# A gated cross-attention and FFN layer: where the first norm's statistics are taken, how the query weights get their mean, and TensorE transposes of the identity at two seams

## The chip, the cores and the metric

The kernel runs on one core of a Trainium2 chip. The metric is the device time of one execution in microseconds. The engines of the core are TensorE (PE: matrix products and transposes), VectorE (DVE), ScalarE (ACT), GpSimd (POOL) and SyncE (SP), which here only issues DMA copies. Each engine works through its own instructions in order and waits on semaphores for the others.

## The reference

x has 4 batches of 1024 tokens of 512 elements, the context 4 batches of 64 tokens. One layer of cross-attention (16 heads of 64) and one quantized feed-forward layer are added, each behind a layer norm and scaled by the tanh of a gate:

```python
scores = einsum('bhqd,bhkd->bhqk', q, k) * SCALE            # q = split(norm(x) @ w_q)
scores = scores + (1.0 - mask) * -10000.0                   # causal: only the first 64 tokens see less
out = softmax(scores) @ v ; return merge(out) @ w_o         # k, v from ctx

x = act_qdq(x)                                              # the FFN: whole-tensor 16 bit levels
up   = act_qdq(x @ lpbq_dequant(w_up).T)                    # weights: 4 bit in blocks of 32
gate = act_qdq(x @ lpbq_dequant(w_gate).T)
sig  = fixed_qdq_u16(sigmoid(gate))
o = act_qdq(act_qdq(gate * sig) * up)
return o @ lpbq_dequant(w_down).T

x = x + tanh(g_xattn[0]) * xattn(layernorm(x), ctx, ctx, ...)
x = x + tanh(g_ffn[0]) * ffn(layernorm(x), ...)
```

The first norm's mean and variance of each token are needed for the attention, the second norm's for the feed-forward layer.

## The kernel before, in words

The 4096 tokens are 32 tiles of 128 (NT), in 8 groups of 4 tiles (NG, GRP) or 16 pairs of tiles (NQ; 4 pairs to a batch). All is in float32.

**Setup (0 to 77 us).** The weights are loaded. As q and k meet only in the scores, the query weights are multiplied into the keys beforehand: for each of 8 pairs of heads (hp), TensorE turns the pair's query weights into PSUM (`query_turned`, L535), DVE takes the mean of each row by batch-norm statistics and an aggregation and writes the difference into `wqT` (L547), and TensorE multiplies by the keys (L566) into five PSUM banks (`ps_mm`), which ACT (10 copies for each hp, L577) and DVE (6, L579) empty into `m_all`. In the same way the values are multiplied into the output weights (`value_matrix`, L605, emptied by ACT at L611 and DVE at L613 into `vwo`). Since the mean is taken out of the query weights, the first norm needs only the factor `rstd1`, one number for each token; it scales the scores inside the softmax. Its statistics (`group_stats`: batch-norm statistics L324 and an aggregation L327 for each tile) come from copies of x, one of 1 MB (`xe`) for each group: groups 0, 1 and 2 behind the head pairs 3, 5 and 6, in the order of the program, groups 3 and 4 among the value products. At L745 `norm_of` turns the variances of groups 0 to 4 into `rstd1`: an addition (L175) for each group and several small instructions on DVE, with a square root on ACT (L178), whose table must be loaded. All that `norm_of` issues has a raised priority.

**Attention (77 to 546 us).** For each pair q, TensorE computes the scores of pair q+1 (seven products, as in Strassen's scheme, L411), and between them turns the weights of pair q (`weights_turned`, L656); it then multiplies these by the values (`attend`, seven products, L690). ACT or DVE add each product into `e` (L417, L419). The softmax takes maxima, exponentials (ACT, L449, 32 for a pair, with a table of its own) and a division (DVE, L455). Four additions on DVE (L662 to L665) prepare the turned weights `eT` for the scheme; L663 is used below as the mark of a pair. `attend` adds its result to the tokens `xg` (L698) and takes the second norm's statistics (L324). `renormed` scales a tile by the second norm (ACT, L718; DVE for the last two, L723), turns it (L731) and keeps it for the next stage. The last pairs of each group end with `norm_of` for the second norm of that group. For groups 5, 6 and 7 the first norm's statistics are taken from `xg` in the pairs 7, 9 and 11, when `xg` has been loaded, and their norm is joined to the second norm's `norm_of` of those pairs. DVE also does the dequantization of the gate and up weights and the sums of the scheme meanwhile.

**Gate (553 to about 870 us), up (to 1146) and down (1151 to 1449).** The three products of the feed-forward layer, with the quantization between them. Before the down stage TensorE turns its weights (`down_turned`, L246; ACT empties each, L248). The largest values over all tokens are needed before a stage's integers can be made. This makes two seams at which TensorE has little to do: between attention and gate, and between up and down.

**The order.** In attention and in the feed-forward layer TensorE's order is that of the program. The other engines' orders are made by a planner from the program and from priorities: `high_priority(SOON)` moves instructions ahead, `issue_after` places them behind a given instruction, `keep_in_program_order` fixes them. Copies into SBUF are issued on SP's queue in that queue's order: a copy whose buffer is not yet free holds the copies behind it.

Of the kernel before, what the change touches and what calls it, by code (L numbers as in the profile page):

```python
# [7 lines left out]
F32 = mybir.dt.float32  # L8
# [9 lines left out]
P = 128  # L18
# [9 lines left out]
def kernel(  # L28
# [253 lines left out]
    def down_turned(psp):  # L282
        for cc in range(IC // 4):
            wdT.append(slot([P, 4, H], f"wdT{cc}"))
            for rc in range(H // P):
# [3 lines left out]
                )  # L289
                yield  # L290


    LO, HI = slice(0, HC // 2), slice(HC // 2, HC)
    LEFT, RIGHT = slice(0, HH), slice(HH, H)
# [27 lines left out]
    def stats(pool, src, dst, tag, in_order=False):  # L322
        st = pool.tile([P, 6], F32, name=f"st_{tag}", tag="st")
        ins = nc.vector.bn_stats(st, src)  # L324
        if in_order:
            tc.keep_in_program_order(ins)
        nc.vector.bn_aggr(dst, st)  # L327

    def group_stats(pool, g, x, in_order=False):
        for i in range(GRP):  # L330
            stats(pool, x[:, i, :], mv1[:, g * GRP + i, :], f"a{g}_{i}", in_order)

    def first_norm(*groups):
        return [(rstd1, None, mv1, of_group(g)) for g in groups]
# [124 lines left out]
    with tc.tile_pool(name="su", bufs=1) as su, tc.tile_pool(  # L459
# [75 lines left out]
        def query_turned(hp):  # L535
            ps = ps_tr.tile([P, 4, P], F32, name=f"ps_wq{hp}", tag="tr")
            for hc in range(HC):
                tc.keep_in_program_order(
                    nc.tensor.transpose(
                        ps[:, hc, :], wq[hp // 4][:, hc, (hp % 4) * P : (hp % 4 + 1) * P], ident  # L540
                    )
                )

            ps = ps.rearrange("p c n -> p (c n)")
            mean = su.tile([P, 2], F32, name=f"mean{hp}", tag="mean", bufs=2)
            stats(su, ps, mean, f"wq{hp}")
            nc.vector.tensor_scalar(  # L547
                wqT[hp // 4][:, hp % 4, :], ps, mean[:, 0:1], None, ALU.subtract
            )

        stats_at = (3, 5, 6)
        query_turned(0)
        left = {}
        for hp in range(HP):
# [29 lines left out]
            if hp in stats_at:  # L584
# [2 lines left out]
                nc.sync.dma_start(out=xe, in_=tokens_of(g))  # L587
                group_stats(su, g, xe, True)

        for b in range(2, B):  # L590
            for k in range(2):
                nc.gpsimd.dma_start(out=m_d[b][k], in_=m_all[b][k])
# [4 lines left out]
        left[0] = score_left(0)  # L597
        for _ in batch_sums(0, 0):
            pass
        def value_matrix(b, hp, ps):  # L600

            for j in range(2):
                half = slice(j * D, (j + 1) * D)
                to = j if b % 2 == 0 else 1 - j
                nc.tensor.matmul(  # L605
                    ps[to * D : (to + 1) * D, :], vT[half, hp, b * KL : (b + 1) * KL],
                    wo[hp // 4][half, hp % 4, :], start=True, stop=True,
                )
            dst = vwo[b][hp // 4][:, hp % 4, :]
            if b != B - 1 or hp % 2 == 0:  # L610
                nc.scalar.activation(dst, ps, AF.Copy, scale=tanh_g[0])  # L611
            else:
                nc.vector.tensor_scalar(dst, ps, tanh_g[0], None, ALU.mult)  # L613

        for hp in range(HP):
            if hp in (0, 3):
                g = 3 + hp // 3
                xe = pa.tile([P, GRP, H], F32, name=f"xe_{g}", tag="e")
                nc.sync.dma_start(out=xe, in_=tokens_of(g))
                group_stats(su, g, xe)  # L620
            for b in range(2, B):
                value_matrix(b, hp, ps_mm.tile([P, H], F32, name=f"ps_vo{b}_{hp}", tag="mm"))
                if hp % 4 == 3:
                    nc.gpsimd.dma_start(out=vwo_d[b][hp // 4], in_=vwo[b][hp // 4])
# [3 lines left out]
    with tc.tile_pool(name="ps_s", bufs=1, space=PSUM) as ps_s, tc.tile_pool(  # L628
# [113 lines left out]

        sg_t, ag = [], []
        last = NT - GRP
        norm_of(pa, first_norm(*range(5)), "a1")  # L745
        load_four(xf, 1, xb, "x")

        def next_left(q):
# [10 lines left out]
        next(firsts)  # L759
        next(firsts)  # L760
        softmax(0, ahead)
        for q in range(NQ):
            b, k = divmod(q, QPB)
            turns = weights_turned(q, ahead)
# [30 lines left out]
                    renormed(t - GRP)  # L795
            if q % 2 == 1 and q // 2 + 2 < NG:
                load_group(q // 2 + 2)
                if q // 2 + 2 > 4:
                    group_stats(pa, q // 2 + 2, xg[q // 2 + 2])
            if q + 1 == NQ:  # L800
                for p in range(UPB - 2):
                    ag.append(weight_sums(wgT, sg_t, p, "g"))
# [1 line left out]
            with tc.issue_after(added):  # L804
                if b + 1 < B and k in (1, QPB - 1):
                    for _ in batch_sums(b + 1, k // 2):
                        pass

            if q == NQ - 2:
                norm_of(pa, [second_norm(slice(last, last + 2))], "c0")  # L810
            if q % 2 == 1 and q + 1 < NQ:
                g = q // 2
                parts = [second_norm(of_group(g))]
                if 4 < g + 2 < NG:
                    parts += first_norm(g + 2)
                norm_of(pa, parts, f"b{g}")

            if 0 < q <= IC:
# [16 lines left out]
        renormed(last + 1)  # L835
        for t in (NT - 1, NT - 2):
            norm_of(pa, [second_norm(slice(t, t + 1))], f"c{t}")
        renormed(NT - 1)
        renormed(NT - 2)
    pools.close()  # L840

    s_x, inv_x = act_scale(over_all([am_x], "x"), None, "x")

    with tc.tile_pool(name="praw", bufs=RAW) as praw, tc.tile_pool(
# [183 lines left out]
        with tc.tile_pool(name="pc", bufs=2) as pc, tc.tile_pool(  # L1028
# [208 lines left out]
            load_early()  # L1237

            turn = down_turned(ps_tr)
            next(turn)  # L1240
            half_of_last(0, 0)
            for step, half, n in zip(tail, ((1, 1), (0, 1), (1, 0)), (1, 0, IC - 2)):
                step()
                half_of_last(*half)
                for _ in range(n):
                    next(turn)


    pe = ctx.enter_context(tc.tile_pool(name="pe", bufs=3))
# [280 lines left out]
```

## Time and profile before

| | us |
|---|---|
| median of 3 runs | 1455.46 (1454.54 to 1455.81) |
| the profiled execution | 1454.49 |
| its span, first to last instruction | 1452.7 |
| TensorE busy | 1395.7 (96%) |
| VectorE busy | 1163.4 (80%) |
| ScalarE busy | 683.2 (47%) |
| GpSimd busy | 96.4 (7%) |
| mean granted TensorE clock | 0.989 |

The page counts the time in which an engine executes; a busy engine may still execute slowly. The views of the waits name, for each engine, the line and buffer that stood, the engine and the line that ended the wait, the total in us, the number and the longest of them. The views of windows give the busy time of each engine in a stretch and, behind them, the granted TensorE clock as a share of full speed, the share of the DMA engines and the GB/s moved.

### The profile page before, as it was taken

The numbers are of one execution on the slowest core, as the hardware profiler recorded it, in microseconds if no ns is written. First come the engines' busy times: TensorE is split into PE (matmuls) and PEld (weight loads), VectorE is DVE, ScalarE is ACT, GpSimd is POOL, SyncE is SP. The second block draws the span as 40 slices with busy tenths as digits, with TensorE's granted clock in tenths as the row PEclk, the third lists the DMA queues.
The fourth block names the chain that finished last, engine by engine and source line by source line (L and its number), as shares of the span: only waits on it lengthen the run. The fifth ranks groups of instructions, "written<-read, shape, count | busy, mean of one in ns | idle before, by whom it ended". The sixth has DMA issues, their size and how long they took to land. (4 is left out here: it accounts for less than half of the span.)

```text
span 1452.7 us, 15275 instructions
## 1 busy us (share of the span) xinstructions
PE 1395.7 (96%) x4816; PEld 847.4 (58%) x4816; DVE 1163.4 (80%) x2165; ACT 683.2 (47%) x1639; POOL 96.4 (7%) x191
## 2 busy tenths in 40 slices
PE   8889999999899988999999999999999899999999
PEld 6526766766567674444444444344444448888887
DVE  3967989898898898799986579888888897666632
ACT  2545786677568852000000049987885532222200
POOL 0000000000000001000000000000000110111110
PEclk9999999999989999999999999999999999999999
DMA  9872344545504315692323448958557475554321
GB/s 282 292 200 68 73 145 108 154 136 116 155 27 123 115 27 214 177 376 87 130 87 116 145 151 340 362 217 318 218 217 260 178 287 174 185 188 173 134 73 44
DMA packets 189513, 249.57 MB, mean 172 GB/s; under 512 B 125300, under 2 KB 125556, under 8 KB 183412
## 3 DMA queue, kind: packets, MB, share of 16 engines
q1 hardware_dynamic: 163956, 146.84, 32.5%
q0 software_dynamic: 18560, 76.56, 13.7%
q10 hardware_dynamic: 6912, 25.17, 4.3%
q8 instruction: 38, 0.62, 0.2%
q14 instruction: 47, 0.39, 0.1%
HBM read 139.47 MB, written 109.05 MB: 171 GB/s over the span
## 5 line engine op out<-in xcount | busy, mean ns | idle before, releaser
L449 ACT ACTIVATE e<-e,mx,rstd 128x64 f32<-128x64 f32 x416 | 177.1, 429 | 8.9 <-DVE mx L447 8.8
L867 PE MATMUL pqup<-t,wuT 128*128 128x512 f32 x192 | 91.1, 597 | 5.1 <-DVE raw_up L888 2.9
L411 PE MATMUL s<-t,xs 128*128 128x512 f32 x192 | 91.7, 600 | 0.2 <-DVE e L419 0.2
L883 ACT COPY raw_gate<-ppgate 128x512 f32<-128x512 f32 x24 | 14.1, 586 | 143.5 <-PE ppgate L867 143.5
L449 ACT ACTIVATION_READ_ACCUMULATOR e<-e,mx,rstd 128x1 f32 x416 | 78.8, 190 | 0.0
L1397 PE MATMUL ep<-wdT,upe 128*128 128x256 f32 x336 | 77.1, 379 | 0.0
L1323 ACT ACTIVATE uie<-upe,inv_up 128x1024 int16<-128x1024 f32 x48 | 53.6, 1144 | 46.7 <-DVE upe L1327 27.4
L419 DVE TENSOR_TENSOR e<-s,e 128x512 f32<-128x512 f32 x80 | 54.6, 682 | 23.4 <-PE s L411 22.9
L1397 PE MATMUL eq<-tw,upe 128*128 128x256 f32 x312 | 72.4, 379 | 0.0
L1397 PEld LDWEIGHTS ep<-wdT,upe 128*128 128x128 f32 x336 | 63.8, 190 | 9.1 <-issue 0.5
L867 PE MATMUL ppup<-xu,wuT 128*128 128x512 f32 x144 | 67.7, 592 | 0.0
L1128 ACT ACTIVATE ar<-raw_up 128x1024 f32<-128x1024 f32 x46 | 48.3, 1053 | 40.1 <-DVE raw_up L1052 40.1
L1061 DVE TENSOR_REDUCE am_gu<-raw_up 128x1 f32<-128x512 f32 x92 | 62.5, 683 | 5.5 <-ACT raw_up L883 4.0
L867 PEld LDWEIGHTS pqup<-t,wuT 128*128 128x128 f32 x192 | 35.6, 189 | 52.6 <-issue 32.5
L411 PE MATMUL s<-m_all,xs 128*128 128x512 f32 x128 | 61.7, 613 | 4.4 <-DVE s_a L183 3.4
L690 PE MATMUL oq<-t,eT 128*128 128x256 f32 x256 | 61.0, 381 | 5.0 <-DVE xg L698 3.7
L875 ACT COPY raw_gate<-ppgate 128x512 f32<-128x512 f32 x24 | 14.1, 586 | 109.2 <-PE ppgate L867 72.7
L1397 PEld LDWEIGHTS eq<-tw,upe 128*128 128x128 f32 x312 | 59.3, 190 | 8.1
L1327 DVE SCALAR_TENSOR_TENSOR upe<-uie,inv_o,gse 128x1024 f32<-128x1024 int16 (+1 forms) x50 | 60.7, 1240 | 3.7 <-ACT uie L1323 3.5
L867 PE MATMUL pqgate<-t,wgTb 128*128 128x512 f32 x128 | 60.2, 592 | 0.0
L411 PEld LDWEIGHTS s<-t,xs 128*128 128x128 f32 x192 | 35.5, 193 | 41.5 <-issue 39.6
L1106 DVE SCALAR_TENSOR_TENSOR q<-gi,inv_gs,si 128x1024 int16<-128x1024 int16 x44 | 56.3, 1281 | 3.6 <-ACT si L1099 2.9
(342 smaller groups left out, 3136.0 us busy)
## 6 DMA issues: line engine op xcount, KB each, us to landing
gate_d<-raw_gate ACTq DMA_DIRECT2D x48, 512.0 KB, 2.6
gt<-gate_d SPq DMA_DIRECT2D x48, 512.0 KB, 4.6
upe<-up_d SPq DMA_DIRECT2D x24, 1024.0 KB, 6.3
up_d<-raw_up POOLq DMA_DIRECT2D x46, 512.0 KB, 3.6
gse<-gsi_d SPq DMA_DIRECT2D x24, 512.0 KB, 4.3
gsi_d<-q SPq DMA_DIRECT2D x44, 256.0 KB, 3.1
wxT<-in_x_dram SPq DMA_DIRECT2D x128, 64.0 KB, 2.8
xg<-in_x_dram SPq DMA_DIRECT2D x8, 1024.0 KB, 5.5
```

The costliest lines, as they stand in the source:

```text
L411: nc.tensor.matmul(bank[at], a[k][:, h, :], b[k][:, h, :], start=start and h == 0, stop=h == HC // 2 - 1, skip_group_check=True,)
L419: nc.vector.tensor_tensor(dst, bank[at], other, add)
L449: nc.scalar.activation(ei[:, h, :], ei[:, h, :], AF.Exp, bias=mx[:, h : h + 1], scale=root, accum_out=sm[:, h : h + 1],)
L690: nc.tensor.matmul(bank[at], a[k][:, h, :], b[k][:, h, :], start=start and h == 0, stop=h == HP // 2 - 1, skip_group_check=True,)
L867: nc.tensor.matmul(bank[at], a[k][:, h, :], b[k][:, h, :], start=start and h == 0, stop=h == HC // 2 - 1, skip_group_check=True,)
L875: nc.scalar.copy(r0[:, 1, :], bank["pp"])
L1061: nc.vector.tensor_reduce(am_gu[:, c, u : u + 1], r[:, c, :], AX.X, ALU.max, apply_absolute_value=True,)
L1106: nc.vector.scalar_tensor_tensor(gsi[u], gi, c_gs, si, ALU.mult, ALU.mult)
L1128: nc.scalar.activation(ar, raw[u], AF.Abs)
L1323: nc.scalar.activation(ui, up[:, i, :], AF.Copy, scale=inv_u)
L1327: ins = nc.vector.scalar_tensor_tensor(o[:, i, w], ui[:, w], c_o, gs[:, i, w], ALU.mult, ALU.mult)
L1397: nc.tensor.matmul(bank[at], a[u // 2][k][:, u % 2, q % 2, :], w_of[u // 2][k][:, u % 2, :], start=start and u == 0, stop=u == UPB - 1, sk ...
```

## The change

It has three parts.

1. **The first norm's statistics.** In setup only groups 0 and 1 are taken, behind head pairs 2 and 5; the norm of group 0 follows the loop over head pairs. A new `stats_of(g)` loads the four tiles of a group by four copies of 256 KB into two rotating buffers `xe` and takes the statistics of each. It is called for groups 2 and 3 behind the last value product that DVE empties (the planner may issue them only after it), and for groups 4 to 7 in the pairs 0 to 3, behind `attend`. The norm of groups 1 to 3 follows the first softmax; that of groups 4 to 7 is joined to the second norm's in pair 5. The statistics from `xg` in the pairs 7, 9 and 11 are gone, so x of the groups 5 to 7 is read once more than before.
2. **The mean of the query weights.** ACT copies the turned weights out of PSUM and sums each row on the way; DVE subtracts the sum over 512, in place.
3. **Transposes of the identity.** `keep_going` issues n TensorE transposes of the 128x128 identity into a PSUM tile which nothing reads: 12, 10 and 18 around the last two `renormed` tiles, and 7, 7 and 14 around the last two turns of the down weights.

TensorE's other instructions keep their order. On DVE, ACT and SP the planner arrives at another order in the setup and in the attention; in the later stages only some of ACT's and SP's instructions at the second seam change places. SP issues 363 rows in place of 336.

```diff
+    def keep_going(ps, n):
+        for _ in range(n):
+            nc.tensor.transpose(ps[:, :P], ident, ident)
...
+    def stats_of(g):
+        for i in range(GRP):
+            xe = pa.tile([P, H], F32, name=f"xe{g}_{i}", tag="xe")
+            nc.sync.dma_start(out=xe, in_=tokens_of(g)[:, i, :])
+            stats(pa, xe, mv1[:, g * GRP + i, :], f"e{g}_{i}")
...
-            ps = ps.rearrange("p c n -> p (c n)")
-            mean = su.tile([P, 2], F32, name=f"mean{hp}", tag="mean", bufs=2)
-            stats(su, ps, mean, f"wq{hp}")
-            nc.vector.tensor_scalar(
-                wqT[hp // 4][:, hp % 4, :], ps, mean[:, 0:1], None, ALU.subtract
+            total = su.tile([P, 1], F32, name=f"total{hp}", tag="total", bufs=2)
+            w = wqT[hp // 4][:, hp % 4, :]
+            nc.scalar.activation(
+                w, ps.rearrange("p c n -> p (c n)"), AF.Copy, accum_out=total
             )
-        stats_at = (3, 5, 6)
+            nc.vector.scalar_tensor_tensor(
+                w, total.to_broadcast([P, H]), -1.0 / H, w, ALU.mult, ALU.add
+            )
+        stats_at = (2, 5)
...
+        norm_of(su, first_norm(0), "a0")
         for b in range(2, B):
...
+                on_vector.append(nc.vector.tensor_scalar(dst, ps, tanh_g[0], None, ALU.mult))
         for hp in range(HP):
-            if hp in (0, 3):
-                g = 3 + hp // 3
-                xe = pa.tile([P, GRP, H], F32, name=f"xe_{g}", tag="e")
-                nc.sync.dma_start(out=xe, in_=tokens_of(g))
-                group_stats(su, g, xe)
...
-        norm_of(pa, first_norm(*range(5)), "a1")
         load_four(xf, 1, xb, "x")
...
         softmax(0, ahead)
+        with tc.issue_after(on_vector[-1].ins):
+            for g in (2, 3):
+                stats_of(g)
+        norm_of(pa, first_norm(1, 2, 3), "a1")
         for q in range(NQ):
...
                 load_group(q // 2 + 2)
-                if q // 2 + 2 > 4:
-                    group_stats(pa, q // 2 + 2, xg[q // 2 + 2])
...
+            if q < NG - 4:
+                stats_of(q + 4)
...
                 parts = [second_norm(of_group(g))]
-                if 4 < g + 2 < NG:
-                    parts += first_norm(g + 2)
+                if q == 5:
+                    parts += first_norm(*range(4, NG))
...
+        idle = ps_s.tile([P, H], F32, name="idle", tag="s0")
+        keep_going(idle, 12)
         renormed(NT - 1)
+        keep_going(idle, 10)
         renormed(NT - 2)
+        keep_going(idle, 18)
...
+            idle = ps_g.tile([P, TB], F32, name="idle_c", tag="pn")
             next(turn)
             half_of_last(0, 0)
             for step, half, n in zip(tail, ((1, 1), (0, 1), (1, 0)), (1, 0, IC - 2)):
                 step()
                 half_of_last(*half)
-                for _ in range(n):
+                for k in range(n):
+                    if k in (IC - 4, IC - 3):
+                        keep_going(idle, 7)
                     next(turn)
+            keep_going(idle, 14)
```

## Prediction

> **What bounds the kernel now.** I read the page first: the busy shares, then the waits of TensorE (PE), then short windows around the largest waits with the granted clock, last VectorE (DVE) instruction by instruction there.
>
> ```profile
> span 1452.7 us, 15275 instructions
> ...
> PE 1395.7 (96%) x4816; PEld 847.4 (58%) x4816; DVE 1163.4 (80%) x2165; ACT 683.2 (47%) x1639; POOL 96.4 (7%) x191
> ```
>
> PE is busy for 96% of the span: 57 us are left in which it does nothing, and its clock. The change leaves PE's products as they are, so it can only win there.
>
> ```profile
> PE ps_xm L731 <- ACT xm L718: 9.2, 1, 9.2
> PE ps_e L656 <- DVE e L455: 5.8, 4, 2.8
> ...
> PE ps_m L566 <- DVE wqT L547: 4.4, 3, 2.8
> ...
> PE s L411 <- DVE s_a L183: 3.4, 1, 3.4
> ...
> PE ps_vo L605 <- DVE vwo L613: 3.1, 2, 1.7
> PE ps_xm L731 <- DVE xm L723: 3.1, 2, 1.7
> ...
> PE ps_vo L605 <- ACT vwo L611: 0.9, 1, 0.9
> ```
>
> In setup PE waits for DVE (wqT, vwo, s_a). The largest wait of the run, 9.2 us from 393.6, stands in pair 10 of the attention, and ACT's xm there waits for DVE: the norm's chain runs from 394.19 (ve_b) to 401.73 (off), behind the statistics of group 7.
>
> ```profile
> 72.78:76.19 3.41, 1.18 (x12) 0.15 (x4) 2.94 (x8) 2.52 (x4) 0.00 (x1) 1.00 1.05 389
> 76.19:83.01 6.82, 5.61 (x7) 2.50 (x8) 1.54 (x9) 1.41 (x3) 1.06 (x2) 0.50 1.06 383
> 393.60:397.04 3.44, 0.00 (x0) 0.00 (x0) 3.44 (x13) 0.44 (x2) 0.00 (x0) 1.00 0.62 195
> 397.04:407.28 10.24, 4.53 (x15) 4.00 (x16) 10.24 (x26) 5.25 (x12) 0.00 (x0) 0.50 0.10 38
> 547.23:550.64 3.41, 0.86 (x6) 0.65 (x7) 3.20 (x15) 0.90 (x3) 0.02 (x1) 1.00 0.20 77
> 550.64:557.47 6.83, 4.75 (x9) 2.13 (x8) 6.21 (x18) 4.42 (x8) 1.08 (x3) 0.50 0.04 16
> 1141.15:1144.56 3.41, 2.82 (x22) 2.07 (x20) 2.72 (x9) 2.91 (x6) 0.37 (x1) 1.00 0.75 294
> 1147.98:1151.39 3.41, 0.69 (x5) 0.46 (x5) 2.11 (x8) 3.30 (x6) 0.57 (x1) 1.00 0.90 309
> 1151.39:1154.80 3.41, 3.41 (x4) 1.47 (x5) 3.38 (x6) 2.75 (x3) 1.65 (x3) 0.50 0.63 111
> ```
>
> The columns: length, busy us of PE, weight loads, DVE, ACT, POOL, then the granted clock. Each stretch at 0.50 follows a window of 3.41 us in which PE was busy for at most 1.18 us (0.35 of it). Two of them are the seams: end of attention (547 to 557) and gate and up into down (1148 to 1155).
>
> ```profile
> 77.00:121.00 44.00, 41.23 (x144) 15.89 (x144) 32.05 (x54) 20.36 (x41) 1.06 (x2) 0.93 0.74 169
> 121.00:229.00 108.00, 106.23 (x423) 72.55 (x424) 91.38 (x181) 76.39 (x289) 4.87 (x9) 1.00 0.36 89
> ```
>
> Here the first four pairs run: DVE has 12.0 and 16.6 us idle. What the change moves there has to fit into that.
>
> **The change, part by part.** The profiled execution took 1454.49 us (span and 1.8 around it), 0.97 under the median of 1455.46; the sum is made against 1454.49 and 0.97 is added. About 0.2% (2.9 us) is what a measurement can tell from no change.
>
> *1. Setup up to scores(0).* Removed from DVE: statistics of groups 2, 3, 4 (12 tiles at 0.69+0.18 = 10.4 us) and, in each of 8 head pairs, statistics and aggregation of the query weights (0.69+0.18); the subtraction (0.75) stays, in place. ACT takes a copy of 128x512 (0.59 for vT) with its row sum (the accumulator read is 0.19): 0.78 x 8 = 6.2 us, beside 16.0 us in which its m_all copies wait. The waits this can end: wqT 2.77+0.19, vwo 1.67+1.48, s_a 3.41, together 9.5; the 0.9 of ACT's vwo comes next, so 8.6 at most. New delays: DVE meets group 0's statistics after head pair 2 (about 37.2), when their 1 MB lands at about 39.3, holding the m_all copies behind them (PE about 1.4, since five banks cover the rest); the norm "a0" puts a table load (1.28) and a square root (0.2) on ACT ahead of a wqT copy (1.5); group 1's statistics (3.5) stand ahead of the last wqT (1.5 after slack). Together 4.4, so scores(0) gains 4.2 to 8.6.
>
> *2. scores(0) to the first turned weights (L663, first pair).* Before 77.4 to 120.5 = 43.1. The first two products took 3.75 and 2.90 us instead of 1.88 at half clock: 2.9 us go if PE no longer idles ahead of them. But DVE gets the 8 tiles of groups 2 and 3 and the norm of groups 1 to 3: two tiles and more fit before the first product ends (DVE idled 6.15 there), the six others (5.2) and the norm (1.5) do not; DVE's idle between reads up to 97 is 2.97+0.38+0.50+1.04 = 4.9. So about 1.8 us fall on PE. Two more table loads (2.6) lie in ACT's 24 idle us. Net 1.2. Steps 1 and 2: gain 5.4 to 9.8; I take 7.5, the middle, as each end rests on one wait.
>
> *3. The pairs.* Pairs 0 to 3 each get four tiles of statistics (4 x 0.87 = 3.5), groups 4 to 7. Pairs 7, 9 and 11 lose as much; the joined norm goes to pair 5. By rows, DVE's work between successive L663 is, before: 15.7, 24.1, 25.9, 23.6, 24.3, 24.0, 29.0, 28.6, 19.5, 22.9, 37.0, 23.8, 18.0, 28.9, 20.1 us; after, in the changed order: 22.2, 24.2, 29.4, 26.0, 27.7, 24.2, 29.7, 25.0, 19.5, 23.7, 29.3, 25.4, 16.9, 28.9, 20.1. PE's own period is 26.7 (25.8 for the first two, 20.1 for the last). With the larger of the two in each, before gives 408.8 (the trace has 413.2, so the order inside pairs costs 4.4 more) and after 403.6: 5.2 won. The long wait of pair 10 also ends its half clock: of 4.53 us of PE work in 397 to 407 half, 2.3, was the clock. I leave 0.6 of waiting there: 5.2+2.3-0.6 = 6.9. Bounds: 11 if the whole 9.2 and 2.3 go and DVE's idle 16.6 takes the new tiles almost free; 2 if each of the first four pairs loses 2 us more, because the softmax chain starts behind a statistic.
>
> *4. The copies.* Five copies of 1 MB become two and 24 of 256 KB (5 to 8 MB) on the sync queue. With two buffers each copy waits for DVE to be done with the one two before, and the queue waits with it: the x and gate weight loads behind it. The x rows of pairs 2 and 3 stand ahead of the first such wait; the others are used a pair (26 us) or more after their place, and 16 issues take 9 to 11 us there. Cost 0; without that slack DVE's first gate tile would stand in front of the softmax.
>
> *5. Seam 1.* 40 transposes around the last two tiles. In the trace 8 transposes take 0.87 us, so these 4.4 us fill a gap that PE waits out anyway (xm: 1.66+1.46). If they hold the clock, 4.75 us of work in 550.64 to 557.47 takes half, 2.4 less; but the second gate product waits for DVE's tile (ends 556.29), so I take 1.0, between 0 and 2.0.
>
> *6. Seam 2.* 28 transposes, 3.1 us, in a window with 0.69 us of work. PE is unbroken from 1151.35 to 1449.3, so all of the first window counts: 3.41 us at half clock, 1.7 less. Against it, 14 transposes (1.5) ahead of a turn may hold it; ACT's turned copy 1150.72 to 1151.30 ends last, so that is covered. The changed order also puts ACT's last turned copy, one uie (1.14 by its row) and SP's gse load ahead of the branch; at most 1.1 us either way for ACT, which was 97% busy in that window (3.30 of 3.41). POOL keeps its order but for one exchanged pair of stores. I take 1.6; bounds -1.5 and 1.7.
>
> In the window 1141.15 to 1144.56 PE did only transposes, and the next windows kept 1.00. The Trainium skill ("TensorE: Matmul & The Clock Gate", Part 4) says that in transpose mode the clock gate doesn't engage as it doesn't count as busy in the same way. By that rule steps 5 and 6 would be worth nothing; the trace's window, at 1.00, speaks against it.
>
> Sum: 7.5+6.9+1.0+1.6 = 17.0. 1454.49-17.0+0.97 = 1438.5.
>
> **Rivals.**
> A. *DVE is full in the first pairs.* For it: 29.4 and 27.7 in my list already pass PE's 26.7, and waits of PE for e-type tiles (5.8) show DVE late. Then step 3 gives 1 and steps 1 and 2 the low 5.4; with 2.6 of the seams 9.0: about 1446.5.
> B. *Transposes don't keep the clock up.* For it: the one window of transposes alone lies between windows of products, so it may have kept their clock, and the few transposes at seam 1 (six PE instructions in 547.23 to 550.64) did not stop the 0.50. Against it: that window itself. Then the 0.50 stays at both seams, and steps 5 and 6 go: 14.4 in place of 17.0, 1441.
> C. *Slower: every new statistic in pairs 0 to 3 falls on PE.* 24 tiles x 0.87 = 20.9 us, if PE always waits for the DVE read behind which a tile stands. Against it stand 28.6 us of idle DVE there. With the low gains (setup 4.2, pair 10 8.2, seams 2.6 = 15.0) the end is 5.9 later: 1461. It decides once more than 15.0 of the 20.9 us land on PE.
> D. *The part in pair 10 does nothing:* the chain of the second norm stays split by other DVE work, and the 9.2 us wait stays. For it: before, 7.5 us of chain held only 1.3 of its own instructions (0.12 to 0.20 each). Step 3 becomes 5.2-(37.0-29.3)+0 = -2.5: the sum is 7.6, about 1448.
> E. *Better:* every high end, 9.8+11+2.0+1.7 = 24.5: 1431.
>
> **How the numbers follow.** Forecast 0.50 (its own range 1432 to 1444), A 0.15, B 0.10, C 0.12, D 0.08, E 0.05. The range 1430 to 1450 takes in the centres of all but C; 0.12 for C and 0.08 for the tails of A, D and E lie outside. Slower by over 0.2%: C but for its mildest sixth, 0.10; within 0.2%: that sixth and the tails of A and D, 0.05; faster by over 0.2%: 0.85.
>
> **What would show it.** PE: no wait for s_a, and scores(0) beginning between 69 and 73; no 0.50 in the 7 us behind it. Pair 10: the wait for ACT's xm below 2 us, no half clock around 400. First pairs: distances of L663 of 25 to 30. Seams: rows "idle" in the windows that read 0.86 and 0.69 of PE work, and 1.00 in the windows after them. Wrong if PE waits for DVE's adds or weights in pairs 0 to 3 in sum by more than 10 us, if the xm wait stays, or if 0.50 stays at both seams.

## The result and the profile after

| | before | after |
|---|---|---|
| median of the runs beside each other (us) | 1455.07 | 1449.02 (1446.81 to 1452.2) |
| ratio, 95% interval | | 0.9956 (0.9943 to 0.997) |
| profiled execution (us) | 1454.49 | 1452.2 |
| its span | 1452.7 | 1450.4 |
| mean granted clock in it | 0.989 | 0.991 |

The kernel became faster by 6.05 us, where 17 were forecast. The profiled execution is the slowest of the five; the other four took 1446.8 to 1450.1 us at a mean clock of 0.993 or 0.994.

TensorE's share on the page of the changed kernel, and its three longest waits between 100 and 540 us (line, tile, who ended them; us in total, times, longest):

```profile
span 1450.4 us, 15457 instructions
...
PE 1406.2 (97%) x4884; PEld 857.6 (59%) x4884; DVE 1155.3 (80%) x2153; ACT 690.7 (48%) x1658; POOL 97.5 (7%) x191
```

```profile
PE oq L702 <- DVE xg L710: 10.0, 4, 4.0
PE ps_e L668 <- DVE e L467: 6.1, 4, 2.8
PE ps_e L668 <- DVE mx L459: 3.3, 1, 3.3
```

In the same stretch the kernel before waits for attend's reads of oq too, but never for long:

```profile
PE oq L690 <- DVE xg L698: 3.7, 4, 1.1
```

The wait of 9.2 us for ACT's xm and the 3.4 for s_a are gone. In their place stand new ones: at attend's third read (oq, 3.6 us in pair 2 and 4.0 in pair 4, the other two 1.2 each) and one of 3.3 us at the turn of pair 1's weights (ps_e). More PE busy time in a shorter span says nothing of itself: 68 of the instructions are the new transposes.

The stretches that count, of the changed kernel (length; busy us of PE, weight loads, DVE, ACT, POOL; granted clock, DMA share, GB/s):

```profile
46.00:49.40 3.40, 1.89 (x12) 1.36 (x14) 3.22 (x12) 2.65 (x13) 0.00 (x0) 0.99 0.99 402
49.40:52.80 3.40, 3.40 (x11) 2.22 (x9) 3.40 (x14) 1.89 (x12) 0.00 (x0) 0.50 0.46 183
135.00:138.20 3.20, 0.60 (x2) 0.00 (x0) 2.56 (x4) 0.95 (x6) 0.00 (x0) 0.99 0.90 127
138.20:145.00 6.80, 6.14 (x15) 3.93 (x16) 2.79 (x6) 5.10 (x20) 0.00 (x0) 0.50 0.60 216
179.20:182.60 3.40, 0.80 (x4) 0.37 (x2) 3.40 (x8) 3.39 (x16) 0.00 (x0) 0.98 0.90 319
182.60:189.40 6.80, 5.81 (x14) 4.64 (x15) 5.97 (x14) 6.80 (x34) 0.54 (x1) 0.51 0.01 2
240.60:244.00 3.40, 0.12 (x1) 0.00 (x0) 3.40 (x7) 3.39 (x12) 0.00 (x0) 0.99 0.83 130
244.00:250.80 6.80, 6.08 (x14) 4.88 (x15) 5.83 (x16) 6.80 (x33) 1.08 (x2) 0.50 0.95 268
547.30:550.70 3.40, 3.05 (x27) 2.62 (x25) 3.23 (x16) 1.51 (x4) 0.54 (x1) 1.00 0.22 80
550.70:554.10 3.40, 2.65 (x23) 2.38 (x22) 2.78 (x10) 1.80 (x3) 0.39 (x1) 1.00 0.00 0
1147.80:1151.20 3.40, 2.41 (x18) 1.97 (x17) 2.46 (x7) 2.73 (x4) 0.65 (x1) 1.00 0.64 238
```

The seams kept 1.00. But three waits of 3.3, 3.6 and 4.0 us in the pairs 1, 2 and 4, which the kernel before does not have, are each followed by 6.8 us at 0.50. In all three windows ahead of that, PE was busy for 0.12 to 0.80 us.

Divided by marks that both traces have (the second addition for the turned weights, L663 before and L675 after; the first turn of the down weights), the two spans compare as follows:

| stretch | before | after | gained | forecast |
|---|---|---|---|---|
| start to scores(0) | 77.41 | 72.40 | 5.0 | 4.2 to 8.6 |
| to the mark of pair 0 | 43.06 | 40.65 | 2.4 | 1.2 |
| marks of pairs 0 to 15 | 413.27 | 421.55 | -8.3 | 6.9 |
| to the first turn of the down weights (seam 1) | 607.01 | 605.76 | 1.25 | 1.0 |
| to the end (seam 2) | 311.95 | 310.04 | 1.9 | 1.6 |

Everything outside the pairs came as forecast, or a little better; the pairs came out 15.2 us worse in this execution. The distances of successive marks (us; a pair's number stands for the stretch from its mark to the next):

| pair | 0 | 1 | 2 | 3 | 4 | 5 | 6 | 7 | 8 | 9 | 10 | 11 | 12 | 13 | 14 |
|---|---|---|---|---|---|---|---|---|---|---|---|---|---|---|---|
| before | 25.2 | 27.1 | 28.7 | 26.8 | 26.6 | 29.3 | 28.8 | 28.1 | 25.7 | 29.6 | 36.3 | 26.2 | 26.4 | 28.2 | 20.1 |
| after | 29.1 | 29.6 | 33.1 | 28.0 | 32.4 | 28.1 | 29.5 | 26.3 | 25.8 | 29.2 | 29.2 | 27.2 | 25.8 | 28.2 | 20.2 |

Pair 10 gives back 7.1, as said. Pairs 0 to 4 lose 17.8.

### The profile page after: what moved, and what is told of

It reads as the page before. It is cut to its first block, busy times and chain, and to the rows that moved or that the text cites. A ratio compares the mean times of both kernels' runs of the same rounds, so it can differ in the third digit from the quotient of the medians.

```text
span 1450.4 us, 15457 instructions
## 1 busy us (share of the span) xinstructions
PE 1406.2 (97%) x4884; PEld 857.6 (59%) x4884; DVE 1155.3 (80%) x2153; ACT 690.7 (48%) x1658; POOL 97.5 (7%) x191
## 3 DMA queue, kind: packets, MB, share of 16 engines
q1 hardware_dynamic: 165828, 149.98, 33.1%
## 5 line engine op out<-in xcount | busy, mean ns | idle before, releaser
L702 PE MATMUL oq<-t,eT 128*128 128x256 f32 x256 | 64.6, 398 | 11.2 <-DVE xg L710 10.0
L702 PEld LDWEIGHTS oq<-t,eT 128*128 128x128 f32 x256 | 50.3, 199 | 20.5 <-DVE xg L710 11.6
L423 PE MATMUL s<-mb,xs 128*128 128x512 f32 x128 | 59.0, 593 | 0.8 <-ACT e L429 0.8
```

The costliest lines, as they stand in the source:

```text
L423: nc.tensor.matmul(bank[at], a[k][:, h, :], b[k][:, h, :], start=start and h == 0, stop=h == HC // 2 - 1, skip_group_check=True,)
L702: nc.tensor.matmul(bank[at], a[k][:, h, :], b[k][:, h, :], start=start and h == 0, stop=h == HP // 2 - 1, skip_group_check=True,)
```

## The experiments

Each ratio is against the kernel before, from runs on the same chip, with its 95% interval. Distances are between the marks above, in the profiled execution of each kernel.

### Each part alone

Three kernels are the one before with a single part of the change, taken whole from the diff.

> The kernel before with part 1 alone (where the first norm's statistics are taken). The changed kernel shows pairs 0 to 14 in 421.6 us against 413.3 before, a loss of 8.3 which is this part's, and a first part (to the first L663) that is 7.4 shorter. If the seams are worth 3.1 and the query mean about 1, this kernel should be some 2 us under before: 1453, between 1450 and 1456. If the loss in the pairs comes from the parts together (an earlier start that only then meets DVE), it would be near 1448 or lower.

> The kernel before with part 2 alone (query mean by ACT's row sums). Theory: in setup DVE sets the end (vwo, s_a), so 8 x 0.9 us less DVE work there moves the first scores up by 2 to 5 us, and the rest stays: 1450 to 1453. Rival: the statistics in program order and the copies of x, not DVE's load, set the setup's end; then within 1 us of before, 1454 to 1456.

> The kernel before with part 3 alone (transposes of the identity at both seams). By the two traces the seams are worth 1.2 and 1.9 us: 1452, between 1451 and 1453, with the half clock gone at 550 and at 1151. Rival (transposes do not keep the clock up): 1455, with both stretches at 0.50 in place.

| | median (us) | ratio |
|---|---|---|
| statistics alone | 1455.67 | 1.0007 (0.9995 to 1.0019) |
| query mean alone | 1451.47 | 0.9985 (0.9974 to 0.9996) |
| transposes alone | 1452.18 | 0.9974 (0.9965 to 0.9984) |

The three deviations add up to -0.34%, the change has -0.44%: the intervals show no dependence of the parts on each other. The statistics' move, on which most of the forecast rested, is worth nothing as a whole: its distances are 28.6, 29.4, 32.1, 28.0, 32.3 in the pairs 0 to 4, and 29.2 in pair 10. The query mean and the transposes make up the gain. With the transposes alone both seams keep their clock (between 550 and 557 and behind 1150):

```profile
550.00:553.40 3.40, 3.01 (x26) 2.56 (x24) 2.77 (x10) 1.45 (x3) 0.38 (x1) 1.00 0.00 0
553.40:556.80 3.40, 1.98 (x5) 0.73 (x5) 3.40 (x8) 3.23 (x6) 0.33 (x1) 1.00 0.01 2
1146.60:1150.00 3.40, 2.05 (x19) 1.84 (x17) 2.10 (x7) 2.68 (x4) 0.57 (x1) 1.00 0.67 230
1150.00:1153.40 3.40, 3.40 (x9) 1.49 (x9) 3.40 (x7) 2.28 (x2) 1.73 (x2) 1.00 0.47 133
```

### What the statistics cost: leaving them out

```diff
-            if q < NG - 4:
-                stats_of(q + 4)
+        nc.vector.memset(mv1[:, 4 * GRP :, :], 1.0)      # in setup
```

> The changed kernel with the 16 statistics of groups 4 to 7 left out (their variances are set to 1 once, so that the softmax of these groups has wrong factors). Theory 1, DVE's load: the stalls in pairs 1, 2 and 4 (3.3, 3.6 and 4.0 us, each with 6.8 us at half clock behind it) go, and the pairs take 403 to 408 us in place of 421.6: a median of 1433 to 1440. Theory 2, DVE's order: the maxima of pair 1 still stand behind other work and at least the stall of pair 1 stays, with its half clock; 1442 to 1449.

Measured: 1440.03 us, 0.9896 (0.9879 to 0.9912), 9.0 under the changed kernel's median. The marks of the pairs take 410.5 in place of 421.6.

```diff
-        with tc.issue_after(on_vector[-1].ins):
-            for g in (2, 3):
-                stats_of(g)
+        nc.vector.memset(mv1[:, 2 * GRP : 4 * GRP, :], 1.0)   # in setup
```

> The changed kernel with the 8 statistics of groups 2 and 3 left out (variances set to 1). It prices step 2: if these statistics put the maxima of pair 1 late, its wait of 3.3 us and half clock go and the time falls by 5 to 7 to 1442 to 1444; if the order of the maxima is the planner's whatever DVE has to do, the stall stays and the time falls by at most 2.

Measured: 1443.33 us, 0.9932 (0.9908 to 0.9957), 5.7 under the changed kernel's median; the marks of the pairs take 413.6.

Waits of PE in the timelines (start, length, instruction, and in brackets the wait ahead of it), first without the late, then without the early statistics:

```profile
139.87 1.57 PE L669 MATMUL ps_e<-ident,e 128*128 128x128 f32 x8 [3.26 <-DVE mx L459]
180.67 1.99 PE L703 MATMUL oq<-t,eT 128*128 128x256 f32 x8 [0.97 <-DVE xg L711]
236.13 1.99 PE L703 MATMUL oq<-t,eT 128*128 128x256 f32 x8 [0.96 <-DVE xg L711]
```

```profile
176.76 3.58 PE L703 MATMUL oq<-t,eT 128*128 128x256 f32 x8 [3.62 <-DVE xg L711]
236.87 3.78 PE L703 MATMUL oq<-t,eT 128*128 128x256 f32 x8 [4.00 <-DVE xg L711]
```

This takes the loss apart. The late statistics make the waits of the pairs 2 and 4 (they are 1.0 without, as in the kernel before: 0.98 and 0.96); the early ones make that of pair 1, with 25.2 and 27.0 for pairs 0 and 1 when they are gone. So neither theory alone holds: pair 1's stall is not the planner's whim, as it goes with the statistics ahead of it, and it is not the late statistics' load. The eight early ones stand ahead of the mark of pair 0 (72.2 to 107.1 us), but cost only 0.4 us there (from scores(0) to the mark 40.7 us, without them 40.3); 6.5 us follow in the pairs 0 and 1. In the medians the 24 statistics cost 9.0 + 5.7 = 14.7 us of the 20.9 that they take on DVE; by the ratios, each against the kernel before on its own chip, it is 8.7 + 3.5 = 12.2. A kernel without either was not run.

### Where in the order? Three tries that did not help

Two statistics a pair in pairs 0 to 7 instead of four in 0 to 3:

```diff
-            if q < NG - 4:
-                stats_of(q + 4)
+            if q < 2 * (NG - 4):
+                stats_of(4 + q // 2, range(2 * (q % 2), 2 * (q % 2) + 2))
...
-                if q == 5:
-                    parts += first_norm(*range(4, NG))
+                if q in (5, 7):
+                    parts += first_norm(q - 1, q)
```

> The changed kernel with the 16 late statistics two a pair in pairs 0 to 7 in place of four a pair in pairs 0 to 3 (norm of groups 4 and 5 with pair 5, of 6 and 7 with pair 7). Theory, the burst: four statistics (3.5 us) in a row of one pair push weight and x work behind L675 and so ahead of attend's reads, and a wait over some 2.5 us then costs 3.4 us of clock more. Two (1.7 us) lengthen the waits of pairs 2 and 4 only to about 2.5 and the half clock behind them goes: 1441 to 1446. Rival, the sum: DVE's work counts wherever it stands, 1447 to 1451.

Raised priority for the maxima:

```diff
-            nc.vector.tensor_reduce(mx, ei, AX.X, ALU.max)
+            with tc.high_priority(SOON):
+                nc.vector.tensor_reduce(mx, ei, AX.X, ALU.max)
```

> The changed kernel with raised priority for the softmax's maxima, so that in pair 1 they stand ahead of the turned weights' additions and of the value sums instead of behind the first attend read. Theory, the order: pair 1's wait of 3.3 us (ps_e) and the half clock behind it go, and the first distance of L675 falls from 29.1 to about 26: 1442 to 1446. Rival, the load: the additions then come later by the two maxima (2.4 us) and PE waits there, no gain: 1447 to 1451.

And both:

> Both together. If burst and order are separate causes their gains add: 1436 to 1442. If one DVE bound stands behind both, no better than the better one.

Measured: 1452.26 (ratio 0.9988, 0.9974 to 1.0002), 1450.76 (0.9975, 0.9961 to 0.9988) and 1451.56 (0.9982, 0.9968 to 0.9996): none better than the change itself. Spread out, the statistics do what the theory of the burst said of the pairs 2 and 4 (the waits there fall to 2.1 us each, and pair 4 to 28.9), but pairs 6 (31.4) and 8 (30.9) lengthen: a read waits 3.2 us in pair 6, and 3.7 us for ACT's xm, up to 347.6, stand at the start of pair 8, behind the norm that is joined in pair 7. So this kernel spreads the statistics and adds a late joined norm, and the spreading alone was not tested. With the maxima first the wait in pair 1 goes, as expected (27.1 for pair 0), but PE now waits for the turned weights in the pairs 0, 2, 3, 4, 6 and 10 (1.6 to 2.7 us each). What is put forward on DVE there pushes something else back on which PE waits as well.

### Pairs with little work, and a norm that is joined

Next I put the statistics into the pairs in which DVE has least to do.

```diff
-            if q < NG - 4:
-                stats_of(q + 4)
+            for g in {3: (4,), 8: (5, 6), 12: (7,)}.get(q, ()):
+                stats_of(g)
+            if q in (8, 12):
+                norm_of(pa, first_norm(*((5, 6) if q == 8 else (7,))), f"d{q}")
...
-                if q == 5:
-                    parts += first_norm(*range(4, NG))
+                if q == 5:
+                    parts += first_norm(4)
```

> The changed kernel with the 16 late statistics in the stretches between two L675 in which DVE has least to do: group 4 with pair 3 (work 22.5 us without it), 5 and 6 with pair 8 (19.5), 7 with pair 12 (16.9), the norms of 5 and 6 and of 7 on their own there. Theory after the last runs: a stretch takes about DVE's work plus 3 us in which DVE waits for PE's attend products, or PE's 25.8 to 26.7 if that is longer; so a statistic is free only where work plus 3 stays under it. Group 4 then costs 1 to 2, pair 8 (19.5+7.0+3 = 29.5 against 25.8) up to 3.5, pair 12 (20.4+3) nothing: pairs 0 to 14 take 414 to 417 in place of 421.6, and the median is 1443 to 1446. Rival: any 16 statistics cost 9 us wherever they stand: 1449 to 1452.

Measured: 1448.06, 0.9956 (0.9941 to 0.9972). Of the eight statistics called in pair 8, five stand in its stretch, which took 25.7, as without them (25.8); three stand in pair 9's, two of them in its first 4 us, and pair 9 took 40.3, with a wait of 5.5 us for the softmax. Pairs 2 and 4 fell to 28.7 and 31.1. The marks take 419.5; the expectation of 414 to 417 was missed by pair 9.

The second kernel moves the early statistics as well and joins the norms of groups 2, 3 and 4 to the second norm's:

```diff
+            for g in {1: (2,), 3: (3,), 5: (4,), 8: (5, 6), 12: (7,)}.get(q, ()):
+                stats_of(g)
...
+                if q in (1, 3, 5):
+                    parts += first_norm(q // 2 + 2)
```

> As the one before, and the early statistics of groups 2 and 3 out of pair 0 as well: group 2 with pair 1, 3 with pair 3, 4 with pair 5, 5 and 6 with pair 8, 7 with pair 12. By the theory pair 0 and the stall of pair 1 fall as in the kernel without the early statistics (3.9 and 2.6 us), and pairs 1, 3, 5 come to 20.7+3.5+3, 22.5+3.5+3, 24.2+3.5+3 = 27.2, 29.0, 30.7 against 27, 27, 28: 1440 to 1445. Rival: 1447 or more.

Measured: 1466.88, 1.0086 (1.0069 to 1.0103), slower than before by 0.9% although the pairs 0 and 1 came to 25.2 and 26.7 as expected. The waits of PE in 100 to 540 us tell why:

```profile
PE ps_xm L743 <- ACT xm L730: 28.1, 3, 9.5
```

That is the wait that the kernel before has once, 9.2 us in pair 10, now three times. In the third kernel each group gets a norm of its own, behind the second norm's:

```diff
-                if q in (1, 3, 5):
-                    parts += first_norm(q // 2 + 2)
...
                 norm_of(pa, parts, f"b{g}")
+            for g in {1: ((2,),), 3: ((3,),), 5: ((4,),), 8: ((5, 6),), 12: ((7,),)}.get(q, ()):
+                norm_of(pa, first_norm(*g), f"d{q}")
```

> The kernel that took 1466.9 us (statistics of groups 2 to 7 with the pairs 1, 3, 5, 8, 12), with one edit: the first norm's factors of groups 2, 3, 4 are made by a norm of their own behind the second norm's instead of in the same one. Theory: there the joined norm lets the second norm wait for statistics that DVE has late, three waits of ACT's xm of 9.3 to 9.5 us with 10.2 us at half clock behind each; alone, they go, and with them 3 x (9.3 + 5.1) less what appears in their place: 1430 to 1445. It would say the same of the 9.2 us in pair 10 of the kernel before. Rival: DVE's order, not the joining, makes xm late; 1460 or more.

Measured: 1452.48, 0.9983 (0.9972 to 0.9993), 14.4 under the joined one, and the waits for xm are gone; the longest that remain in 100 to 540 us are others:

```profile
PE oq L702 <- DVE xg L710: 11.3, 4, 4.2
PE ps_e L668 <- DVE e L467: 9.9, 4, 4.6
```

The square root of the second norm that pair 1 ends with starts at 154.21 us here, and at 164.90 in the joined kernel, behind the aggregation of the first norm's last statistic at 164.05. From the square root to the offset (`off`, for which xm waits) it takes 5.8 us here and 5.7 joined, with other work of DVE in between in both. So it is the joining: `norm_of` makes one square root of both norms, and the second norm, for which TensorE waits at the renormed tiles, is held until DVE has got to the last statistic of the first. The time itself stayed over my 1430 to 1445, as the waits for reads and softmax came back. The change escapes the joined wait in pair 5, since its statistics are done by then.

### The place within a pair

The trace of the changed kernel shows what stands ahead of the read in pair 2 (start, length, line, operands of DVE's instructions):

```profile
177.34 0.41 DVE L710 TENSOR_TENSOR xg<-opn,xg 128x256 f32<-128x256 f32 x1
177.67 0.41 DVE L375 TENSOR_TENSOR xs<-xs 128x256 f32<-128x256 f32 x1
...
178.14 0.42 DVE L376 TENSOR_TENSOR xs<-xs 128x256 f32<-128x256 f32 x1
178.47 0.42 DVE L377 TENSOR_TENSOR xs<-xs 128x256 f32<-128x256 f32 x1
178.81 0.42 DVE L378 TENSOR_TENSOR xs<-xs 128x256 f32<-128x256 f32 x1
179.14 1.21 DVE L449 TENSOR_REDUCE mx<-e 128x16 f32<-128x1024 f32 x1
...
181.93 0.68 DVE L716 TENSOR_TENSOR xg<-xg,r 128x512 f32<-128x512 f32 x1
182.53 0.70 DVE L370 STREAM_TRANSPOSE xs<-wxT 128x512 f32<-128x512 f32 x1
183.16 0.38 DVE L710 TENSOR_TENSOR xg<-oq,xg 128x256 f32<-128x256 f32 x1
```

Between the second and the third read lie 5.8 us of work without a gap (without the late statistics 3.2, from 177.00 to 180.21). The statistics are not among it: they stand before L675 and push the sums of x (xs) behind it. PE needs the third read's bank 1.7 us after the second's. In the kernel before, DVE's idle time in the pairs 1 and 3 (2.8 and 3.1 us) lies among attend's reads, in the first 12 us behind the mark; the change put the statistics of these pairs 21 to 27 us behind it, where DVE had no idle time, and the reads of the pairs 2 and 4 came late. In pair 0 DVE idled for 6.6 us from 14 us behind the mark on, and the late statistics, 13 to 18 us behind it, cost only 0.3. So I left the statistics in the pairs 0 to 3, but put them behind the third read:

```diff
+                if k == 7 and q < NG - 4:
+                    with tc.issue_after(ins.ins), tc.high_priority(SOON):
+                        stats_of(q + 4)
...
-            if q < NG - 4:
-                stats_of(q + 4)
```

(The expectation counts this read, of product 7, as the fourth, with the copy of r as the first.)

> The changed kernel with the 16 late statistics in pairs 0 to 3 still, but behind attend's fourth read (L710, k = 7) at raised priority, so that they stand where DVE idles 1.3 us between two reads. Theory: what makes a statistic cost PE time is that it stands where DVE is dense; in the idle between reads it is free, up to two or three a pair: 1441 to 1445. Rival, the sum of DVE's work: 1448 to 1451.

Measured: 1441.93 us, 0.9907 (0.989 to 0.9923), 7.1 under the changed kernel's median and within 2 of the one that has no late statistics at all. This is the fastest complete kernel of the study. Place and raised priority were not tried apart. In its pair 2:

```profile
180.84 0.38 DVE L710 TENSOR_TENSOR xg<-oq,xg 128x256 f32<-128x256 f32 x1
181.15 1.26 DVE L329 BATCH_NORM_STATS2 st_e<-xe 128x6 f32<-128x512 f32 x2
182.33 0.16 DVE L332 BATCH_NORM_AGGREGATE mv<-st_e 128x2 f32<-128x6 f32 x1
182.41 0.39 DVE L710 TENSOR_TENSOR xg<-opn,xg 128x256 f32<-128x256 f32 x1
```

Two statistics fit between two reads. Its waits in 100 to 540 us:

```profile
PE ps_e L668 <- DVE e L467: 6.9, 5, 2.8
PE oq L702 <- DVE xg L710: 6.2, 4, 1.9
PE ps_e L668 <- DVE mx L459: 3.3, 1, 3.3
```

The longest wait for a read fell from 4.0 to 1.9, and one stretch at 0.50 is left in the first pairs, 6.8 us behind the wait of 3.3 in pair 1 that the early statistics make (a second, 3.4 us at 522.8, is the one that the kernel before has at 530.1). Its marks take 413.3 in place of 421.6. The two stretches of 6.8 us at 0.50 that are gone held 11.9 us of TensorE's work; at half that, by my estimate, the clock is 6 of the 8.3 us. The same for all groups:

```diff
+                if k == 7 and q < NG - 2:
+                    with tc.issue_after(ins.ins), tc.high_priority(SOON):
+                        stats_of(q + 2)
...
-        with tc.issue_after(on_vector[-1].ins):
-            for g in (2, 3):
-                stats_of(g)
-        norm_of(pa, first_norm(1, 2, 3), "a1")
+        norm_of(pa, first_norm(1), "a1")
...
+                if q == 1:
+                    parts += first_norm(2, 3)
```

> As the kernel with the late statistics behind attend's fourth read, and groups 2 and 3 treated in the same way: groups 2 to 7 in the pairs 0 to 5, the norm of 2 and 3 joined to the second norm's of pair 1, that of 4 to 7 to pair 5's. Theory (a statistic is nearly free between attend's reads): pair 0's distance falls from 29.1 to about 26, pair 1's wait of 3.3 us and its half clock go, and the median comes 4 to 6 under 1441.9: 1436 to 1438. Rival: the joined norm of pair 1 waits for the last statistics and holds the second norm; then a wait of xm on ACT of several us appears in pair 2 and the time is 1442 or more.

Measured: 1442.43 us, 0.9917 (0.9897 to 0.9938): no further gain. Pairs 0 and 1 came to 25.2 and 27.6 as expected, and no xm wait appeared; but pair 2 went from 29.5 to 31.9 and pair 6 from 29.0 to 34.4, with a wait of 4.6 us for the third read, where 7.5 us of x, maxima and weight work stand between the second and the third read. No statistic stands in pair 6; why the planner sorted it so there was not tried.

### Putting the read itself first

The third read needs an addition of r (L716) that has no raised priority. If that were the path, raising it should mend all the kernels:

```diff
-                if k == 6:
-                    nc.vector.tensor_tensor(x1[:, RIGHT], x1[:, RIGHT], r, add)
-                if k == 2:
+                with tc.high_priority(SOON):
+                    if k == 6:
+                        nc.vector.tensor_tensor(x1[:, RIGHT], x1[:, RIGHT], r, add)
+                    if k == 2:
...
```

> The changed kernel, its statistics where the change put them, with one edit: attend's two additions of r (L713, L716 here) get the raised priority that the reads of its products (L710) have. Theory: the third read needs L716, so whatever the planner sorts ahead of L716 (maxima, x work, weight work, pushed back by the statistics) stands ahead of the read, and PE waits for its bank (pairs 2 and 4: 3.6 and 4.0 us, then half clock). With L716 early these two waits fall under 1.5 us and their half clock goes: 421.6 less (2.5+3.4) x 2 = 410; the stall of pair 1 stays: 1438 to 1443. Rival: the maxima, now behind, start the exponentials later and PE waits at the turns (ps_e) instead: 1446 to 1450.

> The kernel of 1441.9 us (late statistics behind attend's fourth read) with the same edit. Theory: its remaining waits for L710 (6.2 us in four) fall to some 2: 1436 to 1440. Rival: as above, 1441 or more.

> The kernel of 1442.4 us (groups 2 to 7 behind attend's fourth read in pairs 0 to 5) with the same edit. Theory: its wait of 4.6 us in pair 6 and that of 2.1 in pair 2, with 10.2 us at half clock, go: 1430 to 1436. Rival: 1441 or more.

> The kernel before with the same edit. Its waits for L698 are 3.7 us in four, none with half clock behind it. Theory: the gain is 2 to 4, 1451 to 1454, so the edit mends what the moved statistics did and is not a gain of its own. Rival: it shortens every pair, 1445 or less.

| with L716 first | median (us) | ratio |
|---|---|---|
| the changed kernel | 1458.41 | 1.0026 (1.0014 to 1.0038) |
| late statistics behind the third read | 1454.45 | 1.0 (0.9987 to 1.0012) |
| all statistics behind it | 1455.72 | 0.9999 (0.9986 to 1.0013) |
| the kernel before | 1464.92 | 1.0078 (1.0061 to 1.0095) |

All four lost 9 to 13 us against the same kernel without the edit. The rival had the mechanism right for the changed kernel, but its 1446 to 1450 is 8 us short; of the kernel before, neither the gain that I expected nor the rival's came. The waits of the changed kernel with this edit, 100 to 545 us:

```profile
PE ps_e L668 <- DVE e L467: 18.9, 7, 4.5
PE ps_e L668 <- DVE wam_g L233: 4.6, 1, 4.6
PE ps_e L668 <- DVE mx L459: 3.3, 1, 3.3
```

The waits for the third read are gone, all 10.0 us; but those at the turns (ps_e) grew from 9.4 to 26.8. In the pairs 2, 4 and 10 the maxima come later with the reads first (in pair 2 6.1 and 9.0 us behind the mark, in place of 4.5 and 7.4), with them the exponentials on ACT (32 of 0.43 us, 13.7 a pair), then DVE's division, and then TensorE's turns. In pair 6, with a wait of 3.6 us, the maxima are not later, and its cause was not followed. So after L675 two chains compete for DVE, the reads and the maxima, and either stops TensorE when it is late. The planner's order in the kernel before looks like a balance of the two. A statistic ahead of L675 can delay both; one behind the third read hardly does (third reads wait 1.5 to 1.9 us in the pairs 2, 4 and 6, without late statistics 1.0 to 1.6).

## Why the prediction was right and wrong

The direction and the wide range (1430 to 1450) held, near its upper end; the forecast's own range (1432 to 1444) and the size did not, 6 in place of 17.

- **Steps 1 and 2**: the sum came right, 7.4 gained where 7.5 were taken, with step 1 near its low end (5.0 of 4.2 to 8.6) and step 2 at twice its net (2.4; its terms, 2.9 less 1.8, give 1.1 where 1.2 is written). The delays named for setup came as named: DVE waited 2.2 us for group 0's copy at 39.1, ACT's table load and square root held the norm, and a wqT wait of 1.6 us remained. Behind it lay 3.4 us at half clock, which I had not priced. The copies (step 4) show no wait in the pairs. One term of step 2 failed: it priced the early statistics at 1.8 us, all within its own stretch. They cost 0.4 there and 6.5 in the pairs 0 and 1.
- **Steps 5 and 6** were right: 3.1 where 2.6 were summed, and the transposes alone are worth 2.3 to 5.1 (0.26%, interval 0.16 to 0.35). At the first seam a window of nothing but transposes (547.3, 3.05 of 3.40 us busy) was followed by 1.00. At the second, the window at 1147.8 (2.41 us busy) was too; 0.7 us in it are the down stage's first product, the rest transposes. The Trainium skill ("TensorE: Matmul & The Clock Gate", Part 4) says that in transpose mode the full clock doesn't engage, as it doesn't count as PE-busy in the same way. The transposes of this kernel did count, so for them the measurement decides against that sentence. The rows name them as matrix products, and per column they take about as long as the products (8 of 128 columns in 0.87 us, 4 products of 512 in 1.88), so the trace doesn't show whether that mode was on.
- **Step 3** failed, and in it the sentence "With the larger of the two in each". It took a pair's time to be the larger of PE's period and DVE's work, by which 3.5 us more work in a pair in which DVE had some 3 us to spare is almost free: 5.2 us won over the pairs, with the end of the long wait and its half clock 6.9. Measured were 8.3 lost. Pair 2 took 33.1 with 29.8 us of work on DVE in its trace (29.4 in the prediction), pair 4 32.4 with 28.2 (27.7): the late statistics stood where DVE had no idle time and pushed the third read back. Pair 0 took 29.1 with 22.4 us of work (22.2), through the early statistics; without the late ones it took 28.8. I had the rows to see this (the planner's order was known), but added durations in place of following what each instruction pushes back. The other part of the step, the end of the 9.2 us wait, was right (36.3 to 29.2).
- **The clock** was the second half of that mistake. I counted what ends of half clock, and none that begins. Three new waits of 3.3 to 4.0 us brought 20.4 us at 0.50 in the profiled execution, with 18.0 us of TensorE's work in them; half of it, some 9 us, is my estimate of their cost. The faster executions of the same kernel show a mean clock of 0.993 to 0.994 in place of 0.991; 0.003 of 1450 us is 4.4 us, most of the 5.4 between the fastest and the slowest. That some of the half-clock stretches are missing there is likely from that, but their traces were not seen.
- **The rivals.** D (1448) and A (1446.5) came nearest in number, by luck. A held DVE to be full in the first pairs, and still let step 3 gain 1; DVE was idle for 6.5 us in pair 0, and step 3 lost 8.3. D kept the 9.2 us wait and blamed other DVE work within the norm's chain; in the changed kernel that work still stands there in pair 10 (6.4 us from the square root to the offset, 5.2 before), and the wait is gone. That a joined norm makes such a wait is shown by the joined and the separate norms in other pairs; in pair 10 of the kernel before the joining was not undone alone. C (every new statistic falls on PE), with chance 0.12 against 0.50 for the forecast, came nearest in mechanism, though part of the cost is clock: its limit was 15.0 of 20.9 us, and measured were 14.7 in the medians, 12.2 by the ratios. The kernel gained clearly only as the other parts gave more than C's low ends. B is refuted by the seams. Of the signs named, pair 10, scores(0) and the seams came as said; the distances of 25 to 30 did not (33.1 and 32.4 in the pairs 2 and 4).

## What to carry to other kernels

When work moves to an engine that has idle time on average, look for the instruction ahead of which it lands in that engine's order, and for what this pushes behind the next deadline; sums of durations against a period say little where two chains take turns. In the changed kernel each wait that filled most of a 3.4 us window cost about 3 us more in clock, by the estimate above, so count the waits that begin as well as those that end. A shared small computation (here one norm for two uses) makes the urgent use wait for the late one.

## What was not expected of the hardware

Half clock came also behind a window in which PE was busy for 0.55 of the time (1.89 of 3.40 us, 46.0 to 49.4, short products), where in setup of the kernel before a window with 0.51 (65.95 to 69.36) had kept it. The stretches at half clock begin whole multiples of 3.413 us apart in each trace. With all 19 traces cut into windows on that grid, every window at full clock in which PE was busy for 0.40 of the time or less was followed by half clock (0.06 ahead of the stretch at 244.0 of the changed kernel), and none with 0.55 or more was; between 0.41 and 0.54 both happened (the window of 1.89 us has 0.54 on the grid), and what decides there is open. Windows of transposes alone fall in with this: at 0.56 and more they kept the clock (0.79 at 547.7 in the changed kernel), at 0.50 and less they did not (0.49 at 1142.2 in the kernel with the query mean alone).

One kernel's times spread by 0.4% between executions (1446.8 to 1452.2) along with the mean granted clock (0.994 to 0.991).
